# Layer 0 of a four-layer network: inner channels as 128 plus 64 with two token halves side by side, and a new order of tiles and sums

## The chip, the cores and the metric

The kernel runs on one core of one Trainium2 chip. The metric is the device time of one execution in microseconds. Three runs of the kernel before gave 4215.3, 4217.95 and 4217.99 us; the median is 4217.95. A separate execution under the profiler took 4226.66 us; its instructions span 4224.9 us, at a mean granted TensorE clock of 0.893.

## The reference, cut to what matters

The network has four layers on an input of 4 x 96 x 64 x 64. Only layer 0 is touched by the change. For each of 4 batches it reads the image as a sequence of 4096 tokens with 96 channels and applies two Mamba blocks one after the other, each with 192 inner channels and 16 states per inner channel:

```
h = layernorm(seq); xs, z = split(h @ in_w)            # 192 inner channels each
xc = silu(conv over 4 tokens of xs + conv_b)
dt, Bm, Cm = split(xc @ xproj_w)                       # 6, 16, 16
delta = softplus(dt @ dt_w + dt_b)
dA = exp(delta * A); dBx = delta * Bm * xc             # per inner channel and state
hstates[t] = dA[t] * hstates[t-1] + dBx[t]             # along the tokens
y = (sum over states of hstates * Cm + Dp * xc) * silu(z)
seq = seq + y @ out_w
```

After the two blocks come a 1 x 1 fusion with a pooled vector, a batch normalization over all tokens, and the residual. Layers 1 to 3 (a convolution block, attention with a feed-forward network, a Fourier mixer with a feed-forward network) follow and use the result.

## The kernel before, in words

**Items and tiles.** Layer 0 (`layer0`, from line 93) cuts the 4096 tokens into 4 stretches of T = 1024. The list `items` holds 32 entries: stretch s, block i, batch b. An inner channel and a state make one row of a recurrence, so an item has 192 x 16 = 3072 rows, 24 tiles of 128 rows (32 inner channels by 4 states) by 1024 tokens. The inner channels are held as two halves h of 96, three groups j of 32 in each; g = 0 to 3 is the group of four states. The list `order` gives the sequence of (h, g, j): for each half (0,0), (0,1), (0,2), (3,0), (1,0), (1,1), (1,2), (3,1), (2,0), (2,1), (3,2), (2,2) as (g, j).

**One tile.** ACT computes the decay `da` = exp(nega * ddb) (`exp`, line 463). VectorE (DVE) forms `u` = udb * rep (line 488), where `rep` is Bm spread over 128 rows by a PE product (line 455), and runs the recurrence as one scan (line 492). GpSimd (POOL) multiplies the states by Cm (`times_c`, line 494). PE sums over the states into PSUM tile `y` (`sum_y`, line 511; output 32 rows for each tile, at the rows of group j). Tiles at positions 3, 7, 10, 11 of each 12 are POOL tiles: their product with Bm is made by POOL ahead of time (`times_b`, line 474, at the places in `b_slots`), and their decay, called `dap`, is written into PSUM. rep, u and dap share one PSUM tag of two buffers ("xu"), each of two banks. Two more banks serve as small buffers "ps" for the matmuls of the stage below, and two hold y.

**The written order.** The main loop (lines 553 to 606) runs over m, the number of the tile over all items, t is its place in the item, and fixes by hand the program order on PE, DVE, ACT and POOL. At each m it writes: the scan of m; the decay of m + 1 if that is a POOL tile (its PSUM buffer comes free only then), or rep where a run of non-POOL tiles begins (and rep for m + 2 at t = 2); the decay of m + 3 if that is not a POOL tile (AHEAD = 3); Cm's product of m - 1; a copy of the last state of m - 3 (not in the last stretch); the sums, the gate `y * z` (line 524), the projection and the output copies (`project`, `finish`); and last the steps of the coming item's first stage. Queue order is thus the order of these calls.

**First stage.** `first_stage` (line 230) prepares an item while the one before it runs: its slots 0 to 23 are the 24 tiles of the item before, negative slots lie one item earlier still, slots from 24 on in its own tiles. It holds the normalization (slots -10 to -2), the convolution as PE products into four units (half o, 512 tokens; slots -1 to 2) with an ACT copy of each one slot later, Silu of the whole xc of 96 x 2048 at slot 3 (line 304), the xproj products (6, 7), a split of B and C into three bf16 parts (8 to 11), dt into delta (12 to 14), Softplus (15), z (15 to 17), Silu of z (19). Silu and Softplus need another ACT table than exp and log; `exp_set()` after each of them loads that one back. delta and delta * xc (`du`, on POOL, slots 17 and 22) go through DRAM (dd, ud), so that 32 rows can be loaded four times into 128 (`load_d`); Bm and Cm rows are loaded spread out too (`load_b`, `load_c`). All these transfers are issued by SP, in the order written.

**Output.** `gate` multiplies y by z for one half (96 x 1024) on DVE; `project` adds x and the two halves' output products in PSUM; `finish` copies to SBUF on ACT and, in block 1, takes batch statistics on DVE (line 548).

Of the kernel before, what the change touches and what calls it, by code (L numbers as in the profile page):

```python
# [32 lines left out]
for _name, _w in (  # L33
    [(f"{k}{i}", w) for i in range(2) for k, w in (("ln_g", 1), ("ln_b", 1), ("conv_w", 8), ("conv_b", 2), ("Dp", 2))]
    + [("gp_b", 1), ("fus_b", 1), ("bn_g", 1), ("bn_b", 1)]
    + [("c_b", 1), ("c_ln_g", 1), ("c_ln_b", 1), ("c_b2", 1), ("c_ls", 1)]
    + [("bff", 1), ("f2_b2", 1), ("f3_b2", 1), ("g2", 1), ("be2", 1), ("m2", 1), ("v2", 1)]
):
    V96[_name] = (_n, _w)
    _n += _w  # L40
# [4 lines left out]
for _name, _w in [("A", 48), ("c_b1", 3), ("f2_b1", 3), ("f3_b1", 3), ("id", 48), ("rd", 48), ("rb", 48), ("ib", 48)]:  # L45
    V128[_name] = (_n, _w)
    _n += _w
# [3 lines left out]
class Net:  # L51
# [41 lines left out]
    def layer0(self, dram, scratch):  # L93
        tc, nc, ins = self.tc, self.nc, self.ins
        x_in = ins["x"]
        with ExitStack() as ctx:
# [16 lines left out]
            w_x = cp.tile([C + 1, 2, 2, 4, C], F32, name="w_x")  # L113
            w_z = cp.tile([C + 1, 2, 2, C], F32, name="w_z")
            sel_b = cp.tile([C, 4, 128], BF16, name="sel_bq")
            part = cp.tile([C, 2, C], BF16, name="partq")
            fo = cp.tile([C, 2, C], F32, name="fo")
            dp = cp.tile([C, 2, 2, C], F32, name="dp")
            sel_r = load(cp, "sel_r", [128, 32])
            xproj = load(cp, "xproj", [C, 2, 2, 3 * 2 * NST + DTR])  # L120
# [3 lines left out]
            out_w = load(cp, "out_w", [C, 2, 2, C])  # L124
# [6 lines left out]
            with tc.tile_pool(name="l0s", bufs=1) as wk:  # L131
# [17 lines left out]
                for i in range(2):  # L149
# [6 lines left out]
                    for k in range(4):  # L156
                        nc.vector.tensor_mul(
                            w_x[:, i, :, k, :],
                            ps[:, :DIN].rearrange("p (h c) -> p h c", h=2),
                            rows[:, i, k].rearrange("p (h c) -> p h c", h=2),  # L160
                        )
                    b = bias[C:, i].rearrange("p (h c) -> p h c", h=2)
                    nc.vector.tensor_add(w_x[C:, i, :, 3, :], w_x[C:, i, :, 3, :], b)
                    nc.vector.tensor_copy(w_z[:, i], ps[:, DIN:].rearrange("p (h c) -> p h c", h=2))
                    for h in range(2):
                        nc.vector.tensor_scalar_mul(dp[:, i, h, :], self.ident[:C, :C], self.v(f"Dp{i}", h))
# [3 lines left out]
                owt = load(wk, "out_wt", [C, DIN])  # L170
                for h in range(2):
                    ps = small(C, C)
                    nc.tensor.matmul(ps, owt[:, h * C : (h + 1) * C], fus[:, 0, :], start=True, stop=True)
                    nc.vector.tensor_copy(fo[:, h, :], ps)
# [21 lines left out]
            def mm(ps, w, rhs, start=True, stop=True, shift=0, **kw):  # L196
                for at in halves:
                    at_in = slice(at.start + shift, at.stop + shift)
                    nc.tensor.matmul(ps[:, at], w, rhs[:, at_in], start=start, stop=stop, **kw)  # L199

# [29 lines left out]
            def first_stage(k):  # L230
# [53 lines left out]
                def conv(o, at):  # L284
                    ps = tile_ps()
                    for k in range(4):
                        nc.tensor.matmul(  # L287
                            ps, w_x[:, i, o, k], n[:, at.start + k : at.stop + k], start=k == 0, stop=k == 3
                        )
                    m["xc", o, at.start] = ps  # L290

                def evict(o, at):
                    nc.scalar.copy(m["xc"][:, o, at], m["xc", o, at.start])  # L293

                units = [(o, at) for o in range(2) for at in halves]
                for t, unit in enumerate(units):
                    at_slot(t - 1)(lambda unit=unit: conv(*unit))
                    if t == 0:
                        at_slot(0)(lambda: m.update(xc=wk.tile([C, 2, T], F32, name="xc", tag="xc", bufs=2)))
                    at_slot(t)(lambda unit=unit: evict(*unit))  # L300
# [10 lines left out]
                def _():  # L311
                    m["ps"] = [tile_ps(128), tile_ps(128)]
                    for at, ps in zip(halves, m["ps"]):
                        for h in range(2):
                            nc.tensor.matmul(
                                ps[:nb], xproj[:, i, h], m["xc"][:, h, at], start=h == 0, stop=h == 1
                            )
# [23 lines left out]
                def dt(h):  # L341
                    m["ps"] = [tile_ps(), tile_ps()]
                    for at, ps in zip(halves, m["ps"]):
                        nc.tensor.matmul(ps, dtw[:, i, h * C : (h + 1) * C], dbl[:, at], start=True, stop=True)  # L344

                def dt_out(h):
                    if h == 0:
                        m["delta"] = wk.tile([C, 2, T], F32, name="delta", tag="delta")
                    for at, ps in zip(halves, m["ps"]):
                        nc.scalar.copy(m["delta"][:, h, at], ps)  # L350

                at_slot(12)(lambda: dt(0))
                at_slot(13)(lambda: dt_out(0))
                at_slot(13)(lambda: dt(1))
                at_slot(14)(lambda: dt_out(1))
# [6 lines left out]
                def z_in(o):  # L362
                    m["ps"] = [tile_ps(), tile_ps()]
                    for at, ps in zip(halves, m["ps"]):
                        rhs = n[:, at.start + 3 : at.stop + 3]
                        nc.tensor.matmul(ps, w_z[:, i, o], rhs, start=True, stop=True)  # L366

                def z_out(o):
                    if o == 0:
                        m["z"] = wk.tile([C, 2, T], F32, name="z", tag="z", bufs=2)  # L370
                    for at, ps in zip(halves, m["ps"]):
                        nc.scalar.copy(m["z"][:, o, at], ps)  # L372

                at_slot(15)(lambda: z_in(0))
                at_slot(16)(lambda: z_out(0))
                at_slot(16)(lambda: z_in(1))
                at_slot(17)(lambda: z_out(1))

                @at_slot(16)
                def _():  # L380
                    m["dd"], m["ud"] = [], []
                    for h in range(2):
                        d = dram.tile([C, T], F32, name=f"dd{h}", tag=f"dd{h}", bufs=2)
                        nc.sync.dma_start(d, m["delta"][:, h])
                        m["dd"].append(d)

                def du(h):
                    u = wk.tile([C, T], F32, name="du", tag="du")
                    nc.gpsimd.tensor_mul(u, m["delta"][:, h], m["xc"][:, h])  # L389
                    d = dram.tile([C, T], F32, name=f"ud{h}", tag=f"ud{h}", bufs=2)  # L390
                    nc.sync.dma_start(d, u)
                    m["ud"].append(d)

                at_slot(17)(lambda: du(0))
                at_slot(22)(lambda: du(1))
# [7 lines left out]
                for j in range(3):  # L403
                    at_slot(19)(lambda j=j: load_d(m, "dd", 0, j))
                    at_slot((19, 21, 22)[j])(lambda j=j: load_d(m, "ud", 0, j))
                for g in range(4):
                    at_slot((16, 20, 26, 24)[g])(lambda g=g: load_c(m, g))
                at_slot(20)(lambda: load_b(m, 3))
                at_slot(23)(lambda: load_b(m, 2))
                for j in range(3):  # L410
                    at_slot((23, 30, 31)[j])(lambda j=j: load_d(m, "dd", 1, j))
                    at_slot((27, 33, 34)[j])(lambda j=j: load_d(m, "ud", 1, j))
# [17 lines left out]
            def load_d(made, k, h, j):  # L430

                t = wk.tile([128, T], F32, name=f"{k}b", tag=f"{k}b", bufs=4)
# [9 lines left out]
            half = [(0, 0), (0, 1), (0, 2), (3, 0), (1, 0), (1, 1), (1, 2), (3, 1), (2, 0), (2, 1), (3, 2), (2, 2)]  # L442
            order = [(h, g, j) for h in range(2) for g, j in half]
            pool_tiles = (3, 7, 10, 11)
# [3 lines left out]
            def on_pool(m):  # L448
                return m % 12 in pool_tiles

            def column(t):
                h, g, j = order[t]
                return (h * 3 + j) * 4 + g
# [53 lines left out]
            def start_y(k, h):  # L507
                y = made[k]["y"] = psum_y.tile([C, T], F32, name="y", tag="y")
                mm(y, dp[:, items[k][2], h], made[k]["xc"][:, h])

            def sum_y(k, ts, at):

                for t in ts:
                    j = order[t][2]
                    nc.tensor.matmul(  # L515
                        made[k]["y"][32 * j : 32 * j + 32, at],
                        sel_r,
                        made[k]["hs", t][:, at],
# [5 lines left out]
            def gate(k, h):  # L524
                z = made[k]["z"][:, h, :]
                nc.vector.tensor_mul(z, made[k]["y"], z)

            def project(k):
                b, s, i = items[k]
                x, z = made[k]["x"], made[k]["z"]  # L530
                for at in halves:
                    ps = made[k]["out", at.start] = tile_ps()
                    nc.tensor.matmul(ps, fus[:, 0] if i else self.ident[:C, :C], x[:, at], start=True, stop=False)
                    for h in range(2):
                        w = fo[:, h] if i else out_w[:, 0, h]
                        nc.tensor.matmul(ps, w, z[:, h, at], start=False, stop=h == 1)
# [16 lines left out]
            b_slots = {0: 3, 4: 7, 7: 10, 9: 11, 12: 15, 15: 19, 18: 22, 20: 23}  # L553
            engines = {mybir.EngineType.PE, mybir.EngineType.DVE, mybir.EngineType.Activation, mybir.EngineType.Pool}
            with tc.manual_schedule(engines=engines):
# [3 lines left out]
                for m in range(first, last + 8):  # L559
# [3 lines left out]
                    if 0 <= m + 1 < last:  # L563
                        if on_pool(m + 1):
                            exp(m + 1)

                        if t == 2 and m >= 0:
                            xu_next = rep(m + 2)
                        elif on_pool(m) and not on_pool(m + 1):
                            xu = xu_next if t == 3 and m >= 0 else rep(m + 1)  # L570
# [8 lines left out]

                    for k0 in range(max(k - 1, 0), min(k + 1, len(items))):  # L580
                        for h0 in range(2):
                            at, o = m - 24 * k0 - 12 * h0, 12 * h0
                            if at == 4:
# [858 lines left out]
```

## Time and profile before

| | us |
|---|---|
| median of three runs (range) | 4217.95 (4215.3 to 4217.99) |
| the profiled execution | 4226.66 |
| its span | 4224.9 |
| busy PE / DVE / ACT / POOL | 3488.4 / 3216.6 / 2618.6 / 3024.1 |
| layer 0, first tile to the end of the last item | 83.5 to about 2728 |
| scan (L492), 768 of them | 2.29 to 2.35 each |
| product u (L488), 512 | 1.23 each |
| product with C on POOL (L498), 768 | 2.36 each |
| product with B on POOL (L478), 256 | 2.36 each |

A row of the profile names the line of the code, the engine, the operation, what is written and read with shapes, the count, then busy time, the mean of one, and idle time of the engine just before such instructions with what ended most of it. Where the timeline gives "[... <- ...]", the engine was idle for that time and the name after the arrow is what released it. In a view of waits, a line reads: who waited, for whom, us in total, times, longest.

### The profile page before, as it was taken

The page shows a single profiled execution, that of the slowest core. Times are in us where ns is not written, and L with a number is a line of the kernel's source. Part 1 is how long each engine was busy: PE and PEld are TensorE (multiplying, and loading weights), DVE is VectorE, ACT ScalarE, POOL GpSimd, SP SyncE. Part 2 cuts the span into 40 slices and gives each one's busy share as a digit, 9 for nine tenths or more (in the row PEclk, how much of TensorE's full clock was granted, in tenths as well). Part 3 has the DMA queues.
Part 4 walks back from the last instruction along what each step waited for, and adds up shares of the span by engine and source line. Part 5 has one row for each costly group of instructions (what it writes and reads, how often), then busy time and mean ns, then how long its engine had stood idle before and what let it go on. Part 6 is the DMA issues. An engine that isn't in the chain of part 4 may idle for free. (4 is left out here: it accounts for less than half of the span.)

```text
span 4224.9 us, 39882 instructions
## 1 busy us (share of the span) xinstructions
PE 3488.4 (83%) x11934; PEld 1441.2 (34%) x11934; DVE 3216.6 (76%) x2439; ACT 2618.6 (62%) x4194; POOL 3024.1 (72%) x1619
## 2 busy tenths in 40 slices
PE   6788888877887888888778887579999888887987
PEld 2222222222222222222222222177445426555642
DVE  4999999999999999999999999731222583434649
ACT  4776677676666767676676666322555575544547
POOL 2999999999999999999999999711110274333418
PEclk9889988989898898989889888769999998899989
DMA  6556545555655565465456546373000000000111
GB/s 168 142 141 169 146 132 161 156 150 137 168 146 135 154 165 150 133 165 150 137 154 165 149 130 166 84 216 130 0 0 1 1 1 6 23 28 26 46 41 55
DMA packets 168865, 467.62 MB, mean 111 GB/s; under 512 B 51060, under 2 KB 53150, under 8 KB 165568
## 3 DMA queue, kind: packets, MB, share of 16 engines
q1 hardware_dynamic: 168648, 465.07, 41.0%
q8 instruction: 94, 1.54, 0.2%
q14 instruction: 123, 1.01, 0.1%
HBM read 391.40 MB, written 73.50 MB: 110 GB/s over the span
## 5 line engine op out<-in xcount | busy, mean ns | idle before, releaser
L498 POOL TENSOR_TENSOR hs<-hs,crep 128x1024 f32<-128x1024 f32 x768 | 1794.3, 2355 | 108.6 <-DVE hs L492 83.4
L492 DVE TENSOR_TENSOR_SCAN hs<-da,state,u 128x1024 f32<-128x1024 f32 x384 | 901.6, 2348 | 29.3
L515 PE MATMUL y<-hs,sel_r 128*32 128x512 f32 x3072 | 708.4, 674 | 105.4 <-POOL hs L498 105.3
L488 DVE TENSOR_TENSOR u<-udb,rep 128x1024 f32<-128x1024 f32 x512 | 629.1, 1229 | 47.9 <-PE rep L199 17.4
L472 ACT ACTIVATE dap<-ddb,nega 128x1024 f32<-128x1024 f32 x256 | 285.4, 1115 | 520.1 <-DVE u L488 500.3
L478 POOL TENSOR_TENSOR up<-udb,brep 128x1024 f32<-128x1024 f32 x256 | 604.1, 2360 | 3.7 <-DMA brep<-cd 3.7
L472 ACT ACTIVATE da<-ddb,nega 128x1024 f32<-128x1024 f32 x512 | 581.5, 1141 | 1.0
L287 PE MATMUL ps<-n,w_x 97*96 97x512 f32 x1024 | 469.3, 607 | 1.2 <-DVE n L279 1.2
L492 DVE TENSOR_TENSOR_SCAN hs<-dap,state,up 128x1024 f32<-128x1024 f32 x192 | 445.4, 2331 | 0.0
L515 PEld LDWEIGHTS y<-hs,sel_r 128*32 128x32 f32 x3072 | 138.5, 117 | 616.4 <-issue 405.9
L492 DVE TENSOR_TENSOR_SCAN hs<-da,u 128x1024 f32<-128x1024 f32 x128 | 292.9, 2289 | 9.7
L1021 POOL CAST hq<-y 128x512 fp8e5<-128x512 f16 x192 | 118.4, 642 | 222.4 <-DVE y L1020 222.1
L287 PEld LDWEIGHTS ps<-n,w_x 97*96 97x96 f32 x1024 | 165.7, 165 | 274.6 <-issue 254.2
L199 PE MATMUL rep<-r,sel_bq 96*128 96x512 bf16 x384 | 131.3, 427 | 146.6 <-DVE hs L492 146.5
L344 PE MATMUL ps<-dbl,dtw 103*96 103x512 f32 x256 | 179.8, 841 | 52.5 <-ACT r L335 52.5
L293 ACT COPY xc<-ps 96x512 f32<-96x512 f32 x128 | 74.5, 582 | 231.9 <-PE ps L287 231.9
L366 PE MATMUL ps<-n,w_z 97*96 97x512 f32 x256 | 144.2, 691 | 68.4 <-ACT z L372 68.4
L1169 POOL TENSOR_TENSOR av<-av,ec 128x780 f32<-128x780 f32 x32 | 58.8, 1838 | 197.6 <-ACT av L1166 192.2
L815 POOL TENSOR_TENSOR xc<-xc,rs 96x512 f32<-96x512 f32 x32 | 40.4, 1266 | 208.0 <-ACT rs L814 198.2
L389 POOL TENSOR_TENSOR du<-delta,xc 96x1024 f32<-96x1024 f32 x64 | 150.9, 2357 | 27.8 <-ACT delta L359 23.8
L330 PE MATMUL ps<-r,partq 96*96 96x512 bf16 x128 | 49.3, 436 | 124.3 <-ACT r L335 121.4
L492 DVE TENSOR_TENSOR_SCAN hs<-dap,up 128x1024 f32<-128x1024 f32 x64 | 145.6, 2276 | 2.9 <-ACT dap L472 2.1
(255 smaller groups left out, 6305.4 us busy)
## 6 DMA issues: line engine op xcount, KB each, us to landing
ddb<-dd SPq DMA_DIRECT2D x768, 128.0 KB, 3.8
udb<-ud SPq DMA_DIRECT2D x768, 128.0 KB, 3.2
crep<-cd SPq DMA_DIRECT2D x512, 128.0 KB, 4.2
brep<-cd SPq DMA_DIRECT2D x256, 128.0 KB, 4.3
dd<-delta SPq DMA_DIRECT2D x64, 384.0 KB, 4.0
ud<-du SPq DMA_DIRECT2D x64, 384.0 KB, 5.4
band<-in_band SPq DMA_DIRECT2D x24, 1024.0 KB, 4.8
gt<-in_idft SPq DMA_DIRECT2D x64, 256.0 KB, 2.9
```

Of the source, the lines that this page charges most:

```text
L199: nc.tensor.matmul(ps[:, at], w, rhs[:, at_in], start=start, stop=stop, **kw)
L287: nc.tensor.matmul(ps, w_x[:, i, o, k], n[:, at.start + k : at.stop + k], start=k == 0, stop=k == 3)
L344: nc.tensor.matmul(ps, dtw[:, i, h * C : (h + 1) * C], dbl[:, at], start=True, stop=True)
L366: nc.tensor.matmul(ps, w_z[:, i, o], rhs, start=True, stop=True)
L389: nc.gpsimd.tensor_mul(u, m["delta"][:, h], m["xc"][:, h])
L472: nc.scalar.activation(da, made[k]["dd", h, j], AF.Exp, scale=nega[:, col : col + 1])
L478: nc.gpsimd.tensor_mul(u, made[k]["ud", h, j], made[k]["brep", g])
L488: nc.vector.tensor_mul(u, made[k]["ud", h, j], x)
L492: nc.vector.tensor_tensor_scan(hs[:, 1:], made[k].pop(("da", t)), u, 0.0 if s == 0 else st, ALU.mult, ALU.add)
L498: nc.gpsimd.tensor_mul(hs[:, :T], hs[:, 1:], made[k]["crep", order[t][1]])
L515: nc.tensor.matmul(made[k]["y"][32 * j : 32 * j + 32, at], sel_r, made[k]["hs", t][:, at], start=False, stop=True, skip_group_check=True,)
L1021: nc.gpsimd.tensor_copy(q[:, m, :], y2, saturate=False)
```

## The change

The inner channels of layer 0 are no longer two halves of 96. The first part holds channels 0 to 127 on 128 partitions, for 1024 tokens. The second part holds channels 128 to 191 twice, on partitions 0 to 63 for the first 512 tokens and on partitions 64 to 127 for the other 512. xc, delta and z become tiles of 128 x 1536 in place of 96 x 2048: columns 0 to 1023 are the first part, 1024 to 1535 the second. Weights are laid out to match. The products of the second part are pairs of matmuls with 64 output columns each, into the lower and the upper half of one PSUM buffer:

```diff
+            parts = [[(slice(0, 128), at, slice(0, 128))] for at in halves]
+            parts.append([(slice(128, DIN), at, slice(64 * q, 64 * q + 64)) for q, at in enumerate(halves)])
+                def conv(unit):
+                    ps = m["xc", unit] = tile_ps(128)
                     for k in range(4):
+                        for cols, at, rows in parts[unit]:
+                            nc.tensor.matmul(
+                                ps[rows],
+                                w_x[:, i, k, cols],
+                                n[:, at.start + k : at.stop + k],
...
+                for unit in range(3):
+                    at_slot(unit - 1)(lambda unit=unit: conv(unit))
...
+                    at_slot(unit)(lambda unit=unit: nc.scalar.copy(m["xc"][:, place[unit]], m["xc", unit]))
```

So the convolution has three units (slots -1 to 1) where it had four, delta and z come by the same pattern in two steps (two buffers, then one) at the slots of before, and du is made of one piece of 128 x 1024 (slot 17) and one of 128 x 512 (slot 21). The second part's delta and du are written to DRAM by two transfers each, a half row at a time.

An item still has 24 tiles: 16 of the first part (h = 0, j = 0 to 3), then 8 of the second (h = 1, j = 0, 1). Their order, the POOL tiles, the places of rep, of POOL's products with B and of the sums are new:

```diff
-            half = [(0, 0), (0, 1), (0, 2), (3, 0), (1, 0), (1, 1), (1, 2), (3, 1), (2, 0), (2, 1), (3, 2), (2, 2)]
-            order = [(h, g, j) for h in range(2) for g, j in half]
-            pool_tiles = (3, 7, 10, 11)
+            order = [(0, g, j) for g in (0, 2, 1, 3) for j in range(4)]
+            order = order[:4] + order[4:6] + order[8:12] + order[12:14] + order[6:8] + order[14:16]
+            order += [(1, g, j) for g in (0, 1) for j in range(2)] + [(1, 3, 0), (1, 2, 0), (1, 2, 1), (1, 3, 1)]
+            pool_tiles = (4, 5, 10, 11, 14, 15, 20, 23)
...
-            b_slots = {0: 3, 4: 7, 7: 10, 9: 11, 12: 15, 15: 19, 18: 22, 20: 23}
+            b_slots = {1: 4, 2: 5, 6: 10, 8: 11, 11: 14, 12: 15, 15: 20, 19: 23}
+            sums = {5: [((0, 1, 2, 3), 0)], 7: [((0, 1, 2, 3), 1)], 9: [((4, 5, 6, 7), 0)], 10: [((4, 5, 6, 7), 1)]}
+            sums |= {13: [((8, 10, 9, 11), 0)], 14: [((8, 10, 9, 11), 1)], 17: [((12, 14, 13, 15), 0)]}
+            sums |= {18: [((12, 14, 13, 15), 1)], 22: [((16, 17), 0), ((16, 17), 1), ((18, 19), 0), ((18, 19), 1)]}
+            sums |= {25: [((20, 23), 0), ((20, 23), 1), ((21, 22), 0), ((21, 22), 1)]}
...
                         if on_pool(m + 1):
                             exp(m + 1)
-                        if t == 2 and m >= 0:
-                            xu_next = rep(m + 2)
-                        elif on_pool(m) and not on_pool(m + 1):
-                            xu = xu_next if t == 3 and m >= 0 else rep(m + 1)
+                        elif (t + 1) % NTL in (0, 6, 12, 16, 18, 21):
+                            xu = rep(m + 1)
```

A sum now takes tiles whose outputs lie in four different blocks of 32 rows of y (before, in three). y is started at 3 and 20 (before at 4 and 16), the gate runs at 19 on 128 x 1024 and at 26 on 128 x 512 (before at 14 and 26, both on 96 x 1024), projection and output stay at 28 and 29. The buffers of the loaded delta and du become five each (before four), and the slots of the loads move:

```diff
-                for j in range(3):
-                    at_slot(19)(lambda j=j: load_d(m, "dd", 0, j))
-                    at_slot((19, 21, 22)[j])(lambda j=j: load_d(m, "ud", 0, j))
-                for g in range(4):
-                    at_slot((16, 20, 26, 24)[g])(lambda g=g: load_c(m, g))
-                at_slot(20)(lambda: load_b(m, 3))
-                at_slot(23)(lambda: load_b(m, 2))
-                for j in range(3):
-                    at_slot((23, 30, 31)[j])(lambda j=j: load_d(m, "dd", 1, j))
-                    at_slot((27, 33, 34)[j])(lambda j=j: load_d(m, "ud", 1, j))
+                for j in range(4):
+                    at_slot((19, 19, 20, 21)[j])(lambda j=j: load_d(m, "dd", 0, j))
+                    at_slot((19, 20, 22, 23)[j])(lambda j=j: load_d(m, "ud", 0, j))
+                for g, t in ((0, 20), (1, 22), (2, 25), (3, 27)):
+                    at_slot(t)(lambda g=g: load_c(m, g))
+                at_slot(18)(lambda: load_b(m, 2))
+                at_slot(22)(lambda: load_b(m, 3))
+                for j in range(2):
+                    at_slot((33, 34)[j])(lambda j=j: load_d(m, "dd", 1, j))
+                    at_slot((34, 36)[j])(lambda j=j: load_d(m, "ud", 1, j))
```

Silu of xc stays at slot 3, Softplus at 15 and Silu of z at 19. The numbers of matmuls with sel_r, of scans, of products and of loads per item stay the same.

## The prediction

> **What bounds the kernel now.** I read first the busy time by stage. Columns: stretch and its length, then busy time of PE, PEld, DVE, ACT and POOL (instructions), PE clock, DMA share, GB/s.
> ```profile
> 83.50:742.00 658.50, 541.06 (x1541) 155.61 (x1540) 622.55 (x360) 460.32 (x696) 626.62 (x286) 0.88 0.57 150
> 742.00:1400.00 658.00, 536.68 (x1568) 155.97 (x1567) 632.01 (x360) 458.59 (x694) 630.70 (x289) 0.89 0.57 150
> 2715.00:4224.00 1509.00, 1295.43 (x5672) 805.69 (x5672) 665.43 (x951) 792.21 (x1597) 499.23 (x471) 0.92 0.15 43
> ```
> Layer 0 fills 83 to 2715 us; DVE and POOL are each busy 95 to 96% of it, ACT 70%. The third stretch, layers 1 to 3, is untouched. Layer 0 is 32 items of 24 tiles, some 82 us each. Next, DVE's own waits (us in total, times, longest), between 500 and 2800 us:
> ```profile
> DVE stats L548 <- ACT o L547: 24.6, 16, 2.5
> DVE u L488 <- PE rep L199: 9.6, 12, 1.6
> ```
> DVE hardly waits for anything, and never for POOL's products. Over the whole run the page of L488 puts its waits for rep at 17.4 us. POOL waits for DVE 74.4 us in the same stretch (L498 <- DVE hs L492). So DVE sets the pace, POOL is about 2% behind it, and anything that makes DVE wait in an item is paid 31 or 32 times. Third, the timeline of ACT where two POOL tiles follow each other (tiles 22 and 23 of an item; start, duration):
> ```profile
> 1639.67 1.12 ACT L472 ACTIVATE dap<-ddb,nega 128x1024 f32<-128x1024 f32 x1 [0.74 <-DVE u L488]
> 1640.72 1.13 ACT L472 ACTIVATE da<-ddb,nega 128x1024 f32<-128x1024 f32 x1
> 1641.76 0.17 ACT L505 COPY state<-hs 128x1 f32<-128x1 f32 x1
> 1641.84 0.64 ACT L272 ACTIVATE ps<-ps,eps 96x512 f32<-96x512 f32 x1
> 1642.52 0.57 ACT L273 ACTIVATE ps<-ps 96x512 f32<-96x512 f32 x1
> 1643.01 0.65 ACT L272 ACTIVATE ps<-ps,eps 96x512 f32<-96x512 f32 x1
> 1643.69 0.57 ACT L273 ACTIVATE ps<-ps 96x512 f32<-96x512 f32 x1
> 1644.19 1.10 ACT L472 ACTIVATE dap<-ddb,nega 128x1024 f32<-128x1024 f32 x1
> ```
> The exponential of the second POOL tile stands behind everything written between the two, here 2.4 us of Ln and Exp. DVE does not suffer only because its normalizing product (L279, 1.26 us) lies between those two scans. The third view is what the change must be held against: what else comes to stand between two dap.
>
> **What the Trainium skill says.** "PSUM — Partial Sum Buffer", section "Engine vs sequencer instructions", calls the queues of ScalarE, VectorE and GpSimdE strict FIFO, and says matmuls start and complete in program order; the fence above agrees. "ScalarE: Activation LUTs", "What ACT_TABLE_LOAD costs": an activation with immediate operands takes 186 ns + 0.833 ns per element of a partition. For 2048 that is 1892 ns; the trace has 1911 for each Silu and Softplus (L304, L359, L399), so 1536 elements are an estimated 1466 + 19 = 1.48 us. It prices a table load at 1283 ns, as the trace does, and adds a drain of some 1380 ns that the trace does not show: Silu starts 1.29 us after its load. "TensorEngine Tiling (Array Packing)", "Tiling Modes": 128 rows by 64 columns makes two independent tiles. No matmul of before does this; its sums with 32 columns (L515) run three side by side.
>
> **The change, part by part.** *Counts.* 24 tiles, eight of them on POOL, six rep, as before: 24 scans, 16 DVE products and 32 POOL products of tiles stay at 2.35, 1.23 and 2.36 us.
>
> *DVE, removed.* Two gates of 1024 elements (L526, 1.195 us, 1.12 from start to start) become one of 1024 and one of 512 (nearest row L279: 0.667). That saves 0.58 x 32 = 19 us on the path.
>
> *POOL, ACT, PE, removed.* POOL's second du halves: 1.18 us an item. ACT loses three copies (0.48 each from start to start) and three times 0.43 us: 2.7 us. PE: sums drop from 20 rounds an item to 12 (groups of four different 32-column blocks; a round of three takes 1.06 us in the trace), conv from 16 matmuls of 0.92 us to 8 and 8 halves, delta, z and start_y lose a round each. None is on the path; I count them at nothing, since POOL already waits for DVE. If POOL did not have that slack its 1.18 would be worth at most 38 us.
>
> *PE before tile 6.* Before, rep for tile 8 comes after conv, projection and xproj, and DVE waits for it (17.4 us in all). After, rep for tile 6 follows conv, two rounds of sums, start_y and project. From the first product of an item: conv starts at -2.4 (before: 1645.71 against 1647.83); two units 7.0; sums 2.0; the third unit 3.7; start_y waits for the gate after tile 2 (12.1) and takes 1.9; project 5.8; rep 0.6: 20.4. DVE wants it at 20.4. So about zero, and covered by the next point. Gain 17.4.
>
> *Tile 5, added: the wait that decides.* Tiles 4 and 5 are now both POOL tiles. In slot 3 ACT is given tile 4's dap, tile 6's exponential, a state copy, and then still Silu of the next item with both its table loads; only in slot 4 comes tile 5's dap. Before, only one POOL tile (3) stood here, and its dap was written in slot 2, ahead of Silu. Zero is the end of DVE's product for tile 3, which frees tile 4's buffer. ACT: start 0.09 (1598.54 + 1.23 to 1599.86 for tile 10), dap 1.06, da 1.04, state to load 0.20, load 1.29, Silu 1.49, load 1.29, dap 1.11: sum 7.57, with a semaphore 7.6. DVE: scan 3 at 0.10, scan 4 2.26 later, scan 5 2.28 later: 4.6. No DVE work is written between scans 4 and 5. DVE waits 3.0 us. The last item has no successor's Silu: 31 x 3.0 = 93 us. Queued behind the waiting scan are bn_stats, the product of tile 6 and then, through it, POOL.
> Pairs 10 and 11 have 1.06 us of casts between their dap as before (dap ends at 1604.23, its scan starts at 1604.41); pair 14 and 15 gets two delta copies of about the same length: no wait.
>
> *Tile 18, added.* rep for 18 follows z_in(1), which waits for z's copies, which now stand behind two more exponentials (18 and 19 in place of one). From the end of product 13, ACT: dap 14 and da 16 to 2.2, state and two copies to 3.3, dap 15, da 17, state, one copy, da 18, state to 7.4, load, Softplus, load to 11.4, da 19, state to 12.5, first z copy done 13.1. PE: z_in(1) 1.0 and rep 0.6: 14.8. DVE wants it at 14.3. Wait 0.5; between 0 and 1.8 if PE is slow after its idle time (rep 1.03 in place of 0.59, some L366 twice as long). 31 x 0.5 = 15 us.
>
> *bn_stats* (16 items). ACT's output copies come after tile 5's dap and two exponentials; DVE waits about 0.5 where it waited 1.3 (20.5 in the loop without the last item's pair): 8 us, a gain of 12.
>
> *Tail.* Two rounds of sums and half a gate less after the last scan: 2.5 us gained. Start of the stage: as before.
>
> *Queue of SP and buffers.* Each item writes delta and du in three DMAs each instead of two. A load is four DMAs of about 0.4 us issue. du(0) comes out some 7 us behind tile 17, its write lands 5.4 us later, and udb for the next tile 0 is in about 7 us before use. crep loads move from slots 16, 20, 24, 26 to 20, 22, 25, 27, each after its last reader, so SP waits less for POOL (254.3 us before, from 900 to 2050). Counted at nothing; the cover is those 7 us. POOL's products for tiles 4, 5, 10, 11, 14, 15, 20, 23 come at least 2.4 us before their scans by the same reckoning.
>
> *Sum.* 93 + 15 + 8 added; 19 + 17.4 + 20.5 + 2.5 removed: +57. The profiled execution took 4226.66 us (span 4224.9, 1.8 around it): 4284. It is 8.7 above the median of the runs, 4217.95, so I forecast 4275 for a median.
>
> **Rivals.**
> *A, the forecast*: 4275, chance 0.66. By its own bounds (tile 5 from 2.7 to 3.2 with Silu anywhere between 1.43 and 1.52, tile 18 from 0 to 1.8) 4245 to 4320.
> *B, 64-column halves do not overlap*: then the third conv unit ends 3.7 us later, its eviction on ACT holds tile 4's dap by 1.3 us, and z_in(1) takes 0.9 more. 31 x 2.2 = 68 more: 4343, chance 0.16. For it: no 64-column matmul is in the trace. Against: three 32-column ones overlap nearly fully (six instructions in 1.06 us, 0.592 each), and the skill's two tiles.
> *C, faster*: ACT reaches tile 5's dap in time, its queue not being in the order of the loop as I read it (or Silu's piece far shorter). It decides from 3.0 us: below that each 0.1 us is 3 us, and with none left the sum is 15 + 8 + 3 for rep of tile 6 - 59.4 = -33: 4185. Against: the fence above, in which dap waits behind Ln and Exp. Chance 0.12.
> *D, half of it*: the rest of the reckoning is off so that gains and waits cancel, 4218, chance 0.06.
>
> **How the numbers follow.** A measurement of this kernel can tell about 0.2% (8 us) from no change. Slower: A and B, 0.82. Same: D, 0.06. Faster: C, 0.12. The range leaves out C and D and the top of B: 4236 to 4350. A and B hold most of the chance, on one side, so no second range stands beside it.
>
> **What would show it.** In the profile after, DVE should have a row "hs L492 <- ACT dap L472" of about 90 us in 31 pieces of 3 us, where it now has 2.1; the scan after the second dap of tiles 4 and 5 starts 3 us late each item, with Silu and two table loads on ACT before it. DVE's wait for rep should be near 15 us, all at tile 18; L526 near 60 us in all; POOL busy 38 us less, idle more. The third conv unit should take 3.7 us, not 7.4. I am wrong if DVE's wait for dap is small, if POOL's products make DVE wait, or if rep at tiles 6 or 18 costs over 2 us an item.

## The result, and the profile after

The changed kernel took 4345.93 us (median of 4 runs, 4334.77 to 4348.05) against 4217.97 us of the kernel before (4 runs). The ratio is 1.0294, 95% interval 1.0269 to 1.0318: slower by 128 us. The forecast was slower by 57 us, 4275 us. The profiled execution took 4346.53 us, its span is 4344.8 us (before: 4224.9). Layer 0 ends at about 2850 us where it ended at about 2728; what follows takes some 1495 us in both. So the whole loss lies in layer 0.

Busy time by engine, from the page of the changed kernel:

```profile
PE 3477.4 (80%) x11870; PEld 1366.4 (31%) x11870; DVE 3197.7 (74%) x2439; ACT 2524.0 (58%) x4098; POOL 2992.7 (69%) x1619
```

DVE does 18.9 us less work, POOL 31 us less, ACT 95 us less. The engines work less and the kernel is slower: the time is in waits. What DVE waits for in layer 0 (us in total, times, longest; the line numbers are those of the changed kernel):

```profile
DVE hs L505 <- ACT dap L485: 92.0, 32, 3.1
DVE u L501 <- PE rep L195: 49.8, 43, 1.9
DVE u L501 <- DMA udb<-ud: 33.9, 28, 2.9
DVE stats L563 <- ACT o L562: 11.0, 16, 2.9
DVE z L542 <- PE y L531: 6.0, 1, 6.0
```

Before, four of these five stood at

```profile
DVE u L488 <- PE rep L199: 17.4, 16, 2.0
DVE z L526 <- PE y L515: 6.9, 1, 6.9
DVE u L488 <- DMA udb<-ud: 2.2, 1, 2.2
DVE hs L492 <- ACT dap L472: 2.1, 4, 1.4
```

and bn_stats (`stats`) at 24.6 us. The differences, in the order of the first list, are +89.9, +32.4, +31.7, -13.6 and -0.9, together +139.5; with DVE's 18.9 us less work that is +120.6, and the span grew by 119.9. The loss is accounted for.

The first wait, in the timeline of DVE and then of ACT, tiles 3 to 6 of one item:

```profile
1648.94 2.35 DVE L505 TENSOR_TENSOR_SCAN hs<-da,state,u 128x1024 f32<-128x1024 f32 x1
1651.20 2.33 DVE L505 TENSOR_TENSOR_SCAN hs<-dap,state,up 128x1024 f32<-128x1024 f32 x1
1656.47 2.35 DVE L505 TENSOR_TENSOR_SCAN hs<-dap,state,up 128x1024 f32<-128x1024 f32 x1 [2.94 <-ACT dap L485]
```
```profile
1648.87 1.12 ACT L485 ACTIVATE dap<-ddb,nega 128x1024 f32<-128x1024 f32 x1 [1.86 <-DVE u L501]
1649.93 1.13 ACT L485 ACTIVATE da<-ddb,nega 128x1024 f32<-128x1024 f32 x1
1650.97 0.17 ACT L518 COPY state<-hs 128x1 f32<-128x1 f32 x1
1651.16 1.28 ACT L333 ACT_TABLE_LOAD   x1
1652.45 1.49 ACT L333 ACTIVATE xc<-xc 128x1536 f32<-128x1536 f32 x1
1653.96 1.28 ACT L230 ACT_TABLE_LOAD   x1
1655.25 1.12 ACT L485 ACTIVATE dap<-ddb,nega 128x1024 f32<-128x1024 f32 x1
```

Tile 5's decay starts 6.38 us after tile 4's, with Silu and two table loads (4.05 us) between them; its scan waits 2.94 us. Of the 92.0 us, 91.7 lie at tile 5, in 31 pieces.

The second wait, at tile 18, in the timeline of PE:

```profile
1610.93 1.98 PE L209 MATMUL ps<-n,w_z 97*64 97x512 f32 x4 [5.75 <-ACT z L374]
1612.84 1.03 PE L195 MATMUL rep<-r,sel_bq 96*128 96x512 bf16 x2
```

DVE waits for that rep:

```profile
1613.91 1.23 DVE L501 TENSOR_TENSOR u<-udb,rep 128x1024 f32<-128x1024 f32 x1 [1.74 <-PE rep L195]
```

Of the 49.8 us, 43.3 lie at tile 18, in 31 pieces, and 6.4 at tile 16. z's second step comes after 5.75 us of idle time and takes 1.98 us, rep 1.03. The granted clock in this stretch (the last three columns are clock, DMA share and GB/s) is given beside that of a stretch of the next item, 1685.5 to 1688.8, in which the like pair for delta, starting at 1686.20, takes 1.08 us:

```profile
1610.90:1613.90 3.00, 2.97 (x8) 0.52 (x10) 1.27 (x1) 1.50 (x4) 3.00 (x2) 0.50 0.03 12
1685.50:1688.80 3.30, 2.60 (x15) 0.80 (x16) 3.30 (x3) 3.28 (x7) 3.30 (x2) 1.00 0.00 0
```

The third wait is at tile 3. SP's timeline from du's write on:

```profile
1616.33 0.34 SPq L222 DMA_DIRECT2D ud<-du  x1
1616.72 2.17 SPq L431 DMA_DIRECT2D brep<-cd  x4
1618.93 1.82 SPq L446 DMA_DIRECT2D ddb<-dd  x4
...
1637.07 1.82 SPq L431 DMA_DIRECT2D crep<-cd  x4
1639.10 1.87 SPq L431 DMA_DIRECT2D brep<-cd  x4
1641.36 1.83 SPq L446 DMA_DIRECT2D udb<-ud  x4
```

SP issues without a pause for 27 us. A load of four DMAs takes it 1.7 to 2.3 us, and the load of du for tile 3 is the last of twelve, with the second write of du between them. DVE's product of tile 3 starts at 1647.61, 0.34 us late in this item; over the 27 items in which it waits, it is 1.2 us late on average and 2.9 at most.

### The profile page after: what moved, and what is told of

Its sections match the earlier page's. It is cut to its first block, busy times and chain, and to the rows that moved or that the text cites. A ratio compares the mean times of both kernels' runs of the same rounds, so it can differ in the third digit from the quotient of the medians.

```text
span 4344.8 us, 39483 instructions
## 1 busy us (share of the span) xinstructions
PE 3477.4 (80%) x11870; PEld 1366.4 (31%) x11870; DVE 3197.7 (74%) x2439; ACT 2524.0 (58%) x4098; POOL 2992.7 (69%) x1619
## 5 line engine op out<-in xcount | busy, mean ns | idle before, releaser
L501 DVE TENSOR_TENSOR u<-udb,rep 128x1024 f32<-128x1024 f32 x512 | 628.9, 1228 | 108.1 <-PE rep L195 49.8
L316 PE MATMUL ps<-n,w_x 97*64 97x512 f32 (+1 forms) x1024 | 345.8, 602 | 5.1 <-ACT xc L329 4.2
L531 PEld LDWEIGHTS y<-hs,sel_r 128*32 128x32 f32 x3072 | 128.5, 129 | 607.0 <-issue 372.6
L209 PE MATMUL ps<-n,w_z 97*128 97x512 f32 (+1 forms) x256 | 125.0, 830 | 151.2 <-ACT z L374 151.2
L209 PE MATMUL ps<-dbl,dtw 103*128 103x512 f32 (+1 forms) x256 | 155.8, 899 | 80.9 <-ACT delta L374 54.3
L316 PEld LDWEIGHTS ps<-n,w_x 97*64 97x64 f32 (+1 forms) x1024 | 130.5, 164 | 204.7 <-issue 179.8
L295 PE MATMUL ps<-sq,ones 96*96 96x512 f32 x128 | 112.6, 1030 | 75.7 <-ACT n L289 75.7
L525 PE MATMUL y<-xc,dp 128*128 128x512 f32 x192 | 121.7, 751 | 59.3 <-DVE z L542 59.2
L216 PE MATMUL ps<-xc,xproj 128*102 128x512 f32 x128 | 103.4, 902 | 66.4 <-ACT o L560 33.2
```

The lines of the kernel that those rows point to most:

```text
L209: nc.tensor.matmul(ps[rows], w[:, cols], tokens, start=True, stop=True, skip_group_check=True)
L295: nc.tensor.matmul(ps, self.ones, m["sq"][:, at], start=True, stop=True)
L316: nc.tensor.matmul(ps[rows], w_x[:, i, k, cols], n[:, at.start + k : at.stop + k], start=k == 0, stop=k == 3, skip_group_check=True,)
L501: nc.vector.tensor_mul(u, made[k]["ud", h, j], x)
L525: nc.tensor.matmul(y[:, at], dp[:, items[k][2], h], rhs, start=True, stop=True)
L531: nc.tensor.matmul(made[k]["y"][64 * q + 32 * j : 64 * q + 32 * j + 32] if h else made[k]["y"][32 * j : 32 * j + 32, halves[q]], sel_r, ma ...
```

## The experiments

Theory: three separate waits, each from a place in a queue (ACT's for tile 5, PE's for tile 18, SP's for tile 3). Rivals: a wait only covers another that is due at the same place, so that its removal gains nothing; POOL, the second busiest engine, takes over as the bound. Each kernel is compared with the kernel before on the same chip. The kernel before moves by up to 8 us between the groups of runs, so from one group to another the ratios compare better than the times:

| kernel | time, us | before, us | ratio (95% interval) |
|---|---|---|---|
| changed kernel | 4345.93 | 4217.97 | 1.0294 (1.0269 to 1.0318) |
| e1, Silu in slot 5 | 4265.7 | 4225.62 | 1.0089 (1.0072 to 1.0105) |
| e2, rep ahead of z | 4346.98 | 4225.62 | 1.0290 (1.0273 to 1.0307) |
| e3, three loads of delta in slot 16 | 4346.2 | 4225.62 | 1.0283 (1.0268 to 1.0299) |
| e4, e1 to e3 together | 4296.2 | 4225.62 | 1.0170 (1.0153 to 1.0186) |
| e6, du loads first | 4308.25 | 4219.28 | 1.0219 (1.0196 to 1.0241) |
| e7, e6 and e2 | 4277.37 | 4219.28 | 1.0149 (1.0128 to 1.0169) |
| e8, e7 and e1 | 4197.67 | 4219.28 | 0.9955 (0.9937 to 0.9973) |
| e9, e8 and start_y later | 4285.59 | 4219.28 | 1.0167 (1.0146 to 1.0189) |
| e10, e9 and x earlier | 4180.8 | 4218.45 | 0.9905 (0.9886 to 0.9924) |
| e11, e8 and x earlier | 4197.72 | 4218.45 | 0.9949 (0.9932 to 0.9967) |
| e12, e6 and PE kept busy | 4290.25 | 4218.45 | 1.0172 (1.0150 to 1.0193) |

**e1: Silu behind tile 5.**

```diff
-                @at_slot(3)
+                @at_slot(5)
                 def _():
                     nc.scalar.activation(m["xc"], m["xc"], AF.Silu)
                     exp_set()
```

> The changed kernel with one edit: the Silu of xc is written in slot 5, behind the decay of tile 5 and the output copies, in place of slot 3. Theory (the wait of VectorE for the decay of tile 5, 92 us, is caused by Silu and its two table loads standing ahead of it in ScalarE's queue): that wait falls to under 5 us, and the time falls by 85 to 92, to about 4256. Rival (the wait only hides something else that is late at the same place, rep for tile 6 or the loads of delta and du): the wait moves to PE rep or DMA at tile 6 and later, and the time falls by less than 45, to above 4300.

Measured: 4265.7 us. DVE's waits in e1:

```profile
DVE u L501 <- PE rep L195: 63.5, 67, 3.8
...
DVE hs L505 <- ACT dap L485: 0.3, 1, 0.3
```

The wait for dap fell from 92.0 to 0.3 us; that for rep rose to 63.5 (15.9 of it at tile 6, where there was none), that for udb to 42.0. So the cause of the largest wait is shown. Some 80 of its 92 us came back as time (87 by the ratios), and the rest shows up at rep and udb.

**e2: rep ahead of z's second step.**

```diff
-                at_slot(16)(lambda: z_in(1))
-                at_slot(17)(lambda: out("z", 1))
+                at_slot(17)(lambda: z_in(1))
+                at_slot(18)(lambda: out("z", 1))
```

> The changed kernel with one edit: the second step of z's product is written one slot later (17 in place of 16, its copy 18 in place of 17), so that PE has rep for tile 18 ahead of it. Theory (of the 49.8 us that VectorE waits for rep, 43 are at tile 18 and come from rep standing behind this product, which waits for ScalarE's z copies): the wait for rep falls to under 10 us, the time by about 40, to 4306. Rival (PE is late there because its clock is low, whatever stands ahead of rep): rep is still late by 0.5 us or more at tile 18, and the time falls by less than 20.

Measured: 4346.98 us, no change. The wait for rep fell as the theory had it, but the time did not follow, and it was not the rival either. DVE's waits in e2:

```profile
DVE hs L505 <- ACT dap L485: 91.6, 31, 3.1
DVE u L501 <- DMA udb<-ud: 76.1, 41, 3.3
...
DVE u L501 <- PE rep L195: 4.1, 11, 1.2
```

rep is hardly late any more (49.8 to 4.1), but udb is later by nearly as much (33.9 to 76.1). Tile 18 lies between du's place in POOL's queue and tile 3. What DVE did not lose at 18 it lost at 3, because the loads came when they came. So the wait at tile 18 had covered part of one at tile 3; e7 tests this.

**e3: three loads of delta ahead of du's write.**

```diff
-                    at_slot((19, 19, 20, 21)[j])(lambda j=j: load_d(m, "dd", 0, j))
+                    at_slot((16, 16, 16, 21)[j])(lambda j=j: load_d(m, "dd", 0, j))
```

> The changed kernel with one edit: the loads of delta for j = 0, 1, 2 of the first part are written in slot 16, right behind delta's write to DRAM and ahead of du's, in place of slots 19, 19 and 20. Theory (the 33.9 us that VectorE waits for udb come from SP's queue: from du's write on it has 13 loads of four DMAs to issue at about 1.9 us each, and du for tile 3 is the last): three loads less in that chain are 5.7 us, the wait falls to under 6 us, the time by about 29, to 4317. Rival (the transfers themselves are slow, or POOL makes du too late): the wait stays above 20 us.

Measured: 4346.2 us, udb 34.4 us: no change. The edit did not do what it was meant to. SP's timeline in e3:

```profile
1615.45 0.34 SPq L222 DMA_DIRECT2D ud<-du  x1
1615.89 6.05 SPq L446 DMA_DIRECT2D ddb<-dd  x12
...
1640.43 1.83 SPq L446 DMA_DIRECT2D udb<-ud  x4
```

The three loads stand behind du's write although they are written a slot ahead of it: SP is not among the engines whose order the loop fixes, and the built program has it in another order. From du's write to the last load it is 25.0 us as before the edit. The run says nothing on the theory; it corrects the description of the kernel, which had SP issue in the order written.

**e4: the three together.**

> The changed kernel with the three edits together (Silu of xc in slot 5, the second step of z one slot later, three loads of delta in slot 16). If the three waits are separate and nothing else comes due behind them, their gains add: 4346 - 90 - 40 - 29 = 4187, that is 31 below the kernel before. If POOL is what comes next (its work per item is 79.3 us where VectorE's is 79.7), part of it is given back and the time lies at 4200 to 4230, with VectorE waiting for POOL's products or for y.

Measured: 4296.2 us, above e1 alone (1.0170 against 1.0089). udb 77.6 us, rep 31.0 (19.5 at tile 6), bn_stats 27.9. With e2 moving the wait to udb and e3 doing nothing, e4 had no reason to be better than e1. It is worse by some 30 us, and the traces account for about half of that: DVE's waits for udb, rep and bn_stats come to 136.5 us where they were 119.6 in e1, and PE, ahead of the projection, waits 52.4 us for its x where it waited 21.3, a wait that e9 shows on its own. The rest is not explained.

**e6: the loads of du first.** SP's timeline of e6 has 9 loads from du's write up to the last load of du, where the changed kernel has 12. (The expectation's 10 and 13 count the second write of du with them; the difference of three is the same.)

```diff
-                    at_slot((19, 20, 22, 23)[j])(lambda j=j: load_d(m, "ud", 0, j))
-                for g, t in ((0, 20), (1, 22), (2, 25), (3, 27)):
+                    at_slot((19, 20, 21, 22)[j])(lambda j=j: load_d(m, "ud", 0, j))
+                for g, t in ((0, 20), (1, 23), (2, 25), (3, 27)):
...
-                at_slot(18)(lambda: load_b(m, 2))
-                at_slot(22)(lambda: load_b(m, 3))
+                at_slot(12)(lambda: load_b(m, 2))
+                at_slot(24)(lambda: load_b(m, 3))
```

> The changed kernel with loads moved only: brep for group 2 from slot 18 to 12 (ahead of du's write in SP's queue), du for j = 2 and 3 from 22 and 23 to 21 and 22, ahead of crep for group 1 (22 to 23) and brep for group 3 (22 to 24). Between du's write and the last du load SP then has 10 loads to issue instead of 13. Theory (the 33.9 us that VectorE waits for udb, nearly all at tile 3, are SP's issue time of 1.9 us a load): 5.7 us less, the wait falls under 6 us, the time by 25 to 30, to 4317. Rival (the wait only takes up what the wait for rep at tile 18 leaves, and something third stands behind it): the time falls by less than 10.

Measured: 4308.25 us; rep 49.0 us, dap 92.7, and

```profile
DVE u L501 <- DMA udb<-ud: 1.1, 2, 0.7
```

The third wait is SP's issue time, as the theory has it: only places in SP's queue were changed, and the wait went.

**e7: e6 and the edit of e2.**

> The loads of e6_udb_first and the second step of z one slot later as in e2_rep_first. Moving z alone took the wait for rep from 49.8 to 4.1 us but raised the wait for udb from 33.9 to 76.1, and the time stayed. Theory (both waits end in one chain, POOL's du, its write, SP's loads, tile 3, and VectorE waited for the later of the two): with that chain 5.7 us shorter the wait for rep goes without a new one, rep and udb together under 12 us, the time falls by 65 to 72 from the changed kernel, to about 4277. Rival (a third thing, POOL's own pace, ends there too): udb stays above 30 us and the time above 4310.

Measured: 4277.37 us.

```profile
DVE u L501 <- PE rep L195: 6.2, 13, 0.9
...
DVE u L501 <- DMA udb<-ud: 1.7, 2, 1.0
```

The edit that gave nothing alone gives 31 us (4308.25 to 4277.37) once the loads are in time. This shows that in e2 the one wait had covered the other.

**e8: e7 and Silu in slot 5.**

> e7_udb_rep and Silu of xc in slot 5. Theory: another 80 to 90 off, to about 4192, below the kernel before, with 25 to 45 us left of waits for bn_stats and for rep at tile 6. Rival (POOL, 79.3 us of work in an item, becomes the bound): the time stays above 4215 and VectorE waits for POOL's products or for udb.

Measured: 4197.67 us, 0.9955 of the kernel before: the three waits at tiles 5, 18 and 3 are gone. What is left is dap 3.0, udb 1.4, rep 26.3 (12.7 at tile 6, 13.6 at tile 16) and bn_stats 14.2. POOL does not become the bound; DVE waits for its products 0.8 us.

**e9: the start of y behind rep.**

```diff
-                        if at == 3:
+                        if at == 5:
                             start_y(k0, 0)
```

> e8_udb_rep_silu with the start of y for the first part written at tile 5 behind rep, in place of tile 3 ahead of the projection. PE then reaches the projection and rep for tile 6 about 2 us earlier after the gate. Theory (the wait for bn_stats and for rep at tile 6 that the move of Silu leaves comes from PE's queue): rep at tile 6 under 3 us, bn_stats under 10 us, the time 20 to 25 below e8, about 4170. Rival (ScalarE's queue makes them late): no change against e8 within 8 us.

Measured: 4285.59 us, 88 slower than e8. Neither the theory nor the rival had this. The reason is in PE's timeline of e9:

```profile
1604.52 1.99 PE L549 MATMUL ps<-x,ident 96*96 96x512 f32 x2 [3.58 <-DMA x<-in_x]
1606.31 1.91 PE L216 MATMUL ps<-z,out_w 128*96 128x512 f32 x2
1608.15 2.02 PE L217 MATMUL ps<-z,out_w 64*96 64x512 f32 x2
...
1614.84 0.61 PE L195 MATMUL rep<-r,sel_bq 96*128 96x512 bf16 x2
```

The projection now comes first, and its x is not yet there: it is loaded behind the chain above on SP. PE idles, then runs the projection at about half the clock (0.54 granted, 1.00 in the changed kernel), 10.4 us in place of 5.8, and rep for tile 6 is 5 us late in such items. PE's waits for x come to 98.7 us, DVE's for bn_stats to 65.7 and for rep to 55.4, of it 55.0 at tile 6. So start_y had covered the load, which e10 and e11 test.

**e10: e9 with x loaded earlier.**

```diff
-                        if at == 25:
+                        if at == 20:
                             made[k0]["x"] = load_x(*items[k0])
```

> e9_start_y with x for the projection loaded from tile 20 in place of 25. In e9 PE sat idle 3.6 us for that load, ran the projection and rep for tile 6 at half the granted clock, and VectorE waited 54.5 us for rep at tile 6 and 54.6 for bn_stats. Theory (the loss of e9 is the load of x, which start_y had covered): both waits fall under 12 us, the time to about 4175, some 20 below e8. Rival (start_y in front of the projection is needed to keep PE's clock up): rep at tile 6 stays above 25 us and the time above 4230.

Measured: 4180.8 us, 0.9905 of the kernel before: the fastest of all, 165 us below the changed kernel. In layer 0 DVE's waits are down to

```profile
DVE hs L505 <- ACT dap L485: 11.8, 9, 4.6
...
DVE stats L563 <- ACT o L562: 7.7, 9, 2.9
DVE u L501 <- PE rep L195: 7.6, 14, 0.9
```

and layer 0 ends at 2687 us. The rival that POOL takes over as the bound falls; the other, that a wait covers another, held for e2 and e9. The gain over e8 is 17 us by the medians and 21 by the ratios, where some 20 were expected.

**e11: e8 with x loaded earlier**, start_y in its place.

> e8_udb_rep_silu with only the load of x moved from tile 25 to 20; start_y stays in front of the projection. By the trace of e8 PE does not wait for x there, so nothing should change: 4190 to 4205, rep at tile 6 about 12 us. If the time falls by more than 10 the load was late in some items after all.

Measured: 4197.72 us, as e8; rep at tile 6 still 14.1 us. x was in time in e8. The gain of e10 over e8 is start_y's move, which needs the early x.

**e12: PE kept busy ahead of z's second step.**

```diff
+            zeros = cp.tile([C + 1, 128], F32, name="zeros")
+            nc.vector.memset(zeros, 0.0)
...
                 at_slot(15)(lambda: z_in(0))
+                def keep_warm():
+                    for _ in range(4):
+                        nc.tensor.matmul(
+                            made[k - 1]["y"][:, :MB], zeros, w_x[:, 0, :3].rearrange("p k d -> p (k d)")[:, :MB],
+                            start=False, stop=True, skip_group_check=True,
+                        )
+
+                if k:
+                    at_slot(15)(keep_warm)
                 at_slot(16)(lambda: out("z", 0))
                 at_slot(16)(lambda: z_in(1))
```

> e6_udb_first with four matmuls by a matrix of zeros added to y between the two steps of z (the sum does not change), in PE's idle time of 5.75 us before the second step. The trace gives a granted clock of 0.50 for that step and rep behind it. Theory (the forecast of 0.5 us at tile 18 was too small by the clock: z's pair took 1.98 and rep 1.03 us in place of 1.05 and 0.60): the pair takes about 1.1 us, the wait for rep falls from 49 to about 12 us, the time by 30 to 40 from e6, to about 4275. Rival (a pair of 64 columns from z takes two rounds): it still takes 1.9 us and the wait stays above 35.

Measured: rep 18.8 us (11.2 of it at tile 18, where e6 had 43.6), the time 4290.25, 18 below e6 by the medians (20 by the ratios), where 30 to 40 were expected; the spans of the profiled executions differ by 31.5 (4316.4 to 4284.9). PE's timeline of e12:

```profile
1570.65 3.59 PE L394 MATMUL y<-w_x,zeros 97*128 97x512 f32 x8
1575.01 1.08 PE L211 MATMUL ps<-n,w_z 97*64 97x512 f32 x4 [0.76 <-ACT z L376]
1576.02 0.61 PE L197 MATMUL rep<-r,sel_bq 96*128 96x512 bf16 x2
```

The pair of 64 columns takes 1.08 us, not two rounds. It does so in 29 of the 31 items with the filler; in the other two, with 2.32 us of idle time left ahead of it as in many of the 29, it still took 1.98. So the wait at tile 18 goes in two ways: by taking z out of the place ahead of rep (e7), and for the most part by the clock alone (e12).

## Why the prediction was right in its sign and wrong in its size

**Tile 5 was right.** 93 us forecast, 91.7 measured at tile 5, pieces of 3.0 forecast and 2.86 to 3.13 measured; Silu of 1536 elements was estimated at 1.48 us from "ScalarE: Activation LUTs", section "What ACT_TABLE_LOAD costs", and took 1.48 to 1.49. e1 shows the cause by moving it.

**Tile 18 was mis-sized: 15 us forecast, about 43 measured.** Its mechanism held: the first z copy was forecast to be done 13.1 us after product 13, and z's pair started 13.1 us after it (1696.29 against 1683.18). The failed term is "z_in(1) 1.0 and rep 0.6". They took 1.98 and 1.03, at a granted clock of 0.50, after PE had idled; that the clock is the cause is shown by e12, where the pair mostly takes 1.08 us and tile 18 costs 11.2 us in all, near the 15 forecast. The slow case stood in the bound (1.8 us), and an end near the better one was chosen, although the profile before had evidence for the other: rep at 1.03 us, and a z product (L366) at 1.96 us after 2.13 us of idle time.

**SP's queue was the step that failed outright: nothing forecast, 31.7 us more than before measured.** The sentence was "udb for the next tile 0 is in about 7 us before use [...] Counted at nothing; the cover is those 7 us". For tile 0 it holds: that load is issued by 1622.6, and the tile's product starts at 1635.64. The chain was not followed to its last load, tile 3's, twelfth where tile 0's is the third, with eight loads between them, and the price of a load was 1.6 us (4 x 0.4) where SP took about 1.9. e6 shows the cause by moving the loads. This wait and that at tile 18 are worth 68.6 us by the medians of e7 against the changed kernel (61 by the ratios), and 15 were forecast for both.

**The gains were right, but for the tail.** DVE's gates 18.9 us (forecast 19); rep ahead of tile 6 no longer waits (17.4); bn_stats 13.6 us less (forecast 12). The tail gained about 0.5 us in place of 2.5: from the end of the last scan to the end of the last bn_stats it is 13.7 us before and 13.2 after. rep at tile 6 was "covered by the next point", and so it was: with Silu out of the way it cost 13 to 16 us (e8, e1). In its sum the start of the convolution, -2.4, does not follow from the two times given for it, which are 2.1 apart; nothing hangs on it, since start_y waits for the gate.

**Rival B, at 4343, is as high as the result and is wrong.** The third conv unit takes 3.65 us in the changed kernel, z's pair 1.08 in e12. Pairs of 64 columns overlap, as "TensorEngine Tiling (Array Packing)", section "Tiling Modes", has it; the time is where B put it from other causes, and that B's number fits is chance. C, tile 5 in time, is refuted by the trace. The prediction's sign that it would be wrong, "rep at tiles 6 or 18 costs over 2 us an item", did not show (1.9 at most): the miss lay where no sign had been set. DVE's wait for udb had none. Nor was the wait for rep "all at tile 18": 6.4 us of it are at tile 16.

**Sum.** +57 forecast; +28 for tile 18, +32 for udb and +6 for tile 16 on top, and -3 for tile 5 (89.9 more than before in place of 93), give +120 for the span, as measured; what is left are a few us that cancel. The other 8 us of the 128 are the gap between profiled execution and median: 8.7 us before, which the forecast took to stay, and 0.6 after.

## What to carry to other kernels

When work is put in a new order by hand, write down for every engine what stands between two instructions that the busiest engine needs in close succession; other work there is paid each time round, here 2.94 us for 4.05 us of Silu and table loads, 31 times. Follow a chain of transfers to its last member, with the issue time of each on its queue, and not only to its first. And a wait, or a piece of work, that one edit moves away may have covered another wait: e2 alone gave nothing, e9 alone lost 88 us against e8, and each paid (31 and 17 us) once what stood behind it was moved too.

## What the runs showed of the hardware

- In all 14 items in which z's pair of matmuls came after 5.75 us of idle time, PE's granted clock was 0.50 and the pair took 1.97 to 1.98 us in place of 1.08. Four extra matmuls (eight instructions) ahead of it, 3.59 us of useless work on PE, brought the pair to 1.08 in 29 of 31 items and took 30 us out of DVE's wait for rep (49.0 in e6, 18.8 in e12).
- Two matmuls of 64 output columns into the two halves of the partitions overlap: 16 instructions of the third conv unit took 3.65 us, as long as 8 of 96 columns in the kernel before (L287, 3.68).
- SP takes 0.42 to 0.59 us to issue each DMA of 128 KB in the run of loads shown (1.69 to 2.34 us for four), some 27 us in an item with no pause, while such a DMA lands about 4 us after its issue (median). The place in SP's queue, and not the transfer, made the last load late.
